# Attention scores of seven pairs of query tiles by seven half-size products, on one Trainium2 core

## The chip, the core and the metric

The kernel runs on one NeuronCore of a Trainium2 chip. The core has five engines with instruction queues of their own: TensorE (PE, matrix products; its weight loads are listed apart as PEld), VectorE (DVE), ScalarE (ACT), GpSimd (POOL) and SyncE (SP, which here only issues DMAs). They work out of an on-chip memory (SBUF); products of TensorE land in an accumulator memory (PSUM), of which the attention uses eight banks, each a tile of 128x512 FP32 values. DMA engines move data between SBUF and the large memory (HBM). The metric is the device time of one execution in microseconds (us). Before the change it is 1065.05 us, the median of three runs (1064.25 to 1067.31).

## What is computed

The input x has 2 batches of 2048 rows of 512 values, all FP32. Cut to what matters:

```python
xn = layernorm(x)
z  = layernorm(xn)                               # once more, with gamma and beta
q, k, v = z @ qkv[:, :512], z @ qkv[:, 512:1024], z @ qkv[:, 1024:]
scores  = q @ k.T / sqrt(512)                    # per batch, causal
s = softmax(where(causal, scores, -inf)) @ v @ o_proj + xn
g = silu(moe(xn))                                # 8 experts, the best 2 per row
out = x + s * g
```

The kernel folds the projections, so that "q" below is already multiplied with the key weights and "v" with the output projection: scores are products of q with the normalised rows ("k"), and the attention's output is the product of the exponentials with "v", divided by their sum.

## The kernel before

The work is in stages, one after the other. First the rows are normalised and q and v made (some of it by a seven-product scheme in `seven_products`, L383), and stored in HBM with k. Then the mixture of experts runs over 68 tiles of gathered rows (`experts_step`, L934; its rows y go to HBM). Then comes the attention, which this change is about.

Attention runs over 32 query tiles of 128 rows, in the order `seq` (L810): tiles 15 down to 0 of the first batch, then the second batch's in the order 8, 9, 0, 1, 6, 7, 2, 3, 4, 5, 10 to 15. A position in that order is called s, and positions 2n and 2n+1 are a pair, two neighbouring tiles. Keys come in blocks of 512; a tile needs all whole blocks before its own and a part of its own block. With the keys of four blocks (NBB = 4) a tile needs 1 to 16 groups of 128 keys (`place_keys`, L1079).

The order of all instructions is written out by hand: the schedule is manual, so each engine takes its instructions in the order in which the code issues them. The loop at L1314 goes over the steps s. In step s it issues, in this order: the ends of older tiles (`attended`, L1252, on ACT and DVE; `emit`, L1263, on POOL, with the store on SP), loads of their inputs, the scores of tile s (`chunk_scores`, L961, one per block of keys: four matmuls that accumulate over the four groups of 128 features into a PSUM tile of the pool `ps_a`, five of the banks; then on DVE the causal mask on the last 128 columns and the maximum along the row) mixed with the joins of tile s-1, then the negated maximum (`end_scores`), `combine_p`, `divisor`, `exponentials(s)`, and the product with the values for an older tile.

`exponentials` (L1031) makes the exponentials of a tile on ACT, out of the PSUM tiles into a buffer `pr`, with the row sums. They have to be transposed for the product with v: POOL splits each FP32 block into 16-bit halves (`pu`, L1045), a DMA on SP transposes them (`puT`, L1050), and DVE joins the halves again (`join_p`, L1065) in the tile's buffer `turned[s]`. Tiles with up to three groups of keys are transposed on TensorE instead (`turn_p`).

For the pairs in FAST = (0, 1, 2, 3, 13, 14, 15) the product with the values already goes by seven half-size products in place of eight (Strassen's scheme in Winograd's form): over two rows of tiles, two halves of each pair of key groups, and two halves of the 512 output columns. `combine_v` (L1100) makes the sums of v, `combine_p` (L1114) those of the exponentials, both on DVE; `values_first`, `values_next` and `values_end` (L1161, L1174, L1181) make the products in the three banks of the pool `ps_b` and add them up on DVE. Key groups beyond the 2m that both tiles have in pairs are done in the plain way (`product`, L1083). m is at most 7 before the change. The first half of a pair's values runs two steps after its scores, the second three.

The first steps take over from the experts: the scores of tile 0 are issued before the last five expert steps, `exponentials(0)` in step 0, and the loads of v on SP in steps 0 and 1, into memory that the experts' weights held. `gather_y` (L1230) fetches the experts' rows by index on POOL, `gate` (L1240) weighs them on DVE and puts them through Silu on ACT.

## Time and profile before

| | |
|---|---|
| median of three runs | 1065.05 us |
| profiled execution | 1064.85 us |
| its span, first to last instruction | 1063.1 us |
| TensorE busy | 1047.8 us, 99% of the span |
| VectorE busy | 592.9 us, 56% |
| ScalarE busy | 312.1 us, 29% |
| GpSimd busy | 419.2 us, 39% |
| granted TensorE clock | 0.999 |
| first and last score product | 591.4 and 1019.6 us |

The page has one line per group of instructions: source line, engine, operation, the output and input by the program's names, their shape, the count, then busy time and mean duration, and the idle time before them with what ended it. A product of FP32 operands is issued once in the code and shows as two records on PE: four matmuls of a block are eight records. The records of PE overlap (their ends are modelled), so their mean is longer than the time from one to the next; that time is read from their starts. Timelines give the start and the duration of each instruction or of a run of like ones.

### The profile page before, as it was taken

What the parts mean: (1) busy time and instruction counts of PE and PEld (TensorE: products, weight loads), DVE (VectorE), ACT (ScalarE), POOL (GpSimd) and SP (SyncE); (2) the same over time, 40 slices, a digit from 0 to 9 for tenths busy, and PEclk for the clock granted to TensorE, in tenths of its full rate; (3) what the DMA queues carried; (4) which work ended last, traced back from release to release, by engine and by line L of the source; (5) the groups of instructions that cost most, each with busy time, mean ns of one, the idle gap of its engine ahead of it and who ended that gap; (6) DMA issues with size and microseconds to landing.
All of it is one profiled execution on the core that took longest, in us unless ns stands there. A gap on an engine that the chain in (4) does not pass through costs nothing.

```text
span 1063.1 us, 12108 instructions
## 1 busy us (share of the span) xinstructions
PE 1047.8 (99%) x3578; PEld 619.9 (58%) x3578; DVE 592.9 (56%) x1175; ACT 312.1 (29%) x665; POOL 419.2 (39%) x457
## 2 busy tenths in 40 slices
PE   8999999999999999999999999999999999999998
PEld 3688885444555555555545446676764544547677
DVE  5798885775433333333345338545556568565756
ACT  3222321212332222322355131222333443332330
POOL 2364250003433333333331024244447676773452
PEclk9999999999999999999999999999999999999999
DMA  8699999936999999999885186346568768752451
GB/s 292 187 286 290 284 263 356 338 112 174 221 236 224 228 231 222 234 229 221 216 190 133 35 227 151 92 104 176 125 170 251 251 189 228 196 152 72 113 138 39
DMA packets 300511, 209.32 MB, mean 197 GB/s; under 512 B 234520, under 2 KB 247576, under 8 KB 299424
## 3 DMA queue, kind: packets, MB, share of 16 engines
q1 hardware_dynamic: 281248, 146.12, 55.2%
q0 software_dynamic: 10560, 35.17, 12.7%
q10 hardware_dynamic: 8640, 27.27, 7.1%
q8 instruction: 30, 0.49, 0.2%
q14 instruction: 33, 0.27, 0.1%
HBM read 92.89 MB, written 60.03 MB: 144 GB/s over the span
## 4 chain that ended last, share of the span: by engine, by line
PE 82%; DMA 4%; issue 4%; POOL 4%; DVE 3%; ACT 2%; SPq 1%; ACTq 0%; POOLq 0%; DVEq 0%
PE ps L966 18%; PE ph L882 15%; PE py L921 15%; PE p L1140 10%; PE p L400 7%; PE po L1087 5%; PE pj L341 3%; PE pj L346 3%; PE pw L207 2%; PE p L1087 2%; DMA puT<-pu 1%; DMA zuT<-zu 1%; POOL yg L1234 1%; POOL pu L1045 1%; DMA v<-v_d 1%
## 5 line engine op out<-in xcount | busy, mean ns | idle before, releaser
L966 PE MATMUL ps<-k,q 128*128 128x512 f32 (+3 forms) x640 | 239.1, 529 | 0.0
L966 PEld LDWEIGHTS ps<-k,q 128*128 128x128 f32 x640 | 117.2, 190 | 119.7 <-issue 109.8
L921 PE MATMUL py<-w,ht 128*128 (+3 forms) x408 | 187.0, 593 | 0.0
L882 PE MATMUL ph<-w,xT 128*128 (+1 forms) x544 | 173.1, 460 | 0.7 <-POOL keep L1004 0.7
L1045 POOL COPY pu<-pr 128x1024 uint16<-128x1024 uint16 (+2 forms) x74 | 80.0, 1111 | 171.9 <-ACT pr L1038 149.4
L929 DVE COPY y<-py 128x512 f32<-128x512 f32 x68 | 46.9, 689 | 177.7 <-PE py L921 177.7
L907 ACT ACTIVATE ht<-ht,b1sel 128x128 f32<-128x128 f32 (+3 forms) x237 | 73.1, 375 | 231.2 <-DVE ht L901 231.2
L882 PEld LDWEIGHTS ph<-w,xT 128*128 128x128 f32 (+1 forms) x544 | 97.4, 181 | 74.1 <-issue 35.2
L892 POOL COPY hu<-h 128x704 uint16<-128x704 uint16 x68 | 52.2, 768 | 206.9 <-ACT h L890 151.9
L921 PEld LDWEIGHTS py<-w,ht 128*128 128x128 f32 (+3 forms) x408 | 73.5, 182 | 75.3 <-issue 37.6
L768 POOL DMA_INDIRECT xs<-zu_d,toki x68 | 69.0, 1014 | 69.3 <-DVE toki L642 57.9
L1038 ACT ACTIVATE pr<-ps,nm 128x512 f32<-128x512 f32 (+3 forms) x80 | 49.0, 620 | 148.3 <-DVE ri L1218 126.2
L972 DVE TENSOR_REDUCE mx<-ps 128x1 f32<-128x512 f32 (+3 forms) x80 | 48.6, 608 | 69.9 <-PE ps L966 68.7
L1234 POOL DMA_INDIRECT yg<-y_d,posi x64 | 67.9, 1062 | 40.4 <-DVE g L1245 23.4
L1087 PE MATMUL po<-v,pT 128*128 128x512 f32 x182 | 81.2, 593 | 1.1 <-ACT pT L1063 1.1
L264 POOL COPY zu<-z 128x1024 uint16<-128x1024 uint16 x32 | 35.2, 1099 | 77.1 <-DVE z L249 77.1
L1069 DVE COPY pT<-puT 128x1024 uint16<-128x1024 uint16 (+2 forms) x74 | 54.2, 740 | 20.0 <-DMA puT<-pu 20.0
L1087 PEld LDWEIGHTS po<-v,pT 128*128 128x128 f32 x182 | 34.2, 190 | 39.5 <-issue 36.1
L1258 DVE SCALAR_TENSOR_TENSOR o<-xo,xscale,o 128x512 f32<-128x512 f32 x30 | 26.9, 906 | 50.0 <-ACT o L1255 43.0
L842 DVE COPY xT<-xhT 128x1024 uint16<-128x1024 uint16 x68 | 46.5, 684 | 13.4 <-DMA xhT<-xs 8.4
L413 DVE TENSOR_TENSOR so<-p,so 128x512 f32<-128x512 f32 x70 | 45.7, 685 | 14.1 <-DMA v_d<-so 8.0
L1266 POOL TENSOR_TENSOR o<-o,g 128x512 f32<-128x512 f32 x30 | 41.3, 1377 | 14.8 <-DVE o L1258 14.6
(219 smaller groups left out, 1447.8 us busy)
## 6 DMA issues: line engine op xcount, KB each, us to landing
y_d<-y SPq DMA_DIRECT2D x68, 256.0 KB, 3.7
zu_d<-zu SPq DMA_DIRECT2D x32, 264.0 KB, 6.4
x<-in_x_dram SPq DMA_DIRECT2D x32, 256.0 KB, 5.4
kt_d<-kT ACTq DMA_DIRECT2D x8, 1024.0 KB, 5.1
k<-kt_d SPq DMA_DIRECT2D x32, 256.0 KB, 4.2
q<-qt_d SPq DMA_DIRECT2D x32, 256.0 KB, 3.8
v<-v_d SPq DMA_DIRECT2D x32, 256.0 KB, 5.2
xo<-in_x_dram SPq DMA_DIRECT2D x32, 256.0 KB, 3.3
```

What stands on the lines that cost most here:

```text
L400: nc.tensor.matmul(ps[:, r, :], lhsT=lhs[:, c, ts(r, P)], rhs=rhs[:, c, :], start=(c == 0), stop=(c == 1),)
L768: nc.gpsimd.indirect_dma_start(out=xs, out_offset=None, in_=zu_d, in_offset=bass.IndirectOffsetOnAxis(ap=toki[:, i : i + 1], axis=0),)
L882: nc.tensor.matmul(ph[at, :], lhsT=xT[:, c, at], rhs=rhs[k], start=(c == 0), stop=(c == ND - 1),)
L892: nc.gpsimd.tensor_copy(hu[:, :, :H], h.bitcast(U16).rearrange("p (d h) -> p h d", h=2))
L907: nc.scalar.activation(ht[:hn, c, at], ht[:hn, c, at], AF.Silu, bias=b1sel[:hn, c, j : j + 1])
L921: nc.tensor.matmul(py[at, :], lhsT=ht[:k, c, at], rhs=rhs[n], start=(c == 0), stop=(c == NH - 1),)
L966: nc.tensor.matmul(ps[:, :w], lhsT=aqs[seq[s] // 2][:, c, ts(t % 2, P)], rhs=aks[first + j][:, c, :w], start=(c == 0), stop=(c == ND - 1),)
L1045: nc.gpsimd.tensor_copy(pu[:, : 2 * w].rearrange("p (h d) -> p h d", h=2), pr[:, :w].bitcast(U16).rearrange("p (d h) -> p h d", h=2),)
L1069: nc.vector.tensor_copy(turned[s][:, j * TB : j * TB + w].bitcast(U16).rearrange("p (i t h) -> p i t h", t=P, h=2), halves[s][j][:, : 2 * ...
L1087: nc.tensor.matmul(dst, lhsT=turned[s][:, ts(k, P)], rhs=avs[first + k // BT][:, k % BT, cols], start=(start and k == k0), stop=(k == k1 - 1),
L1140: nc.tensor.matmul(dst, lhsT=a[:, k], rhs=v(k), start=(k == 0), stop=(stop and k == n - 1))
L1234: nc.gpsimd.indirect_dma_start(out=y, out_offset=None, in_=y_d, in_offset=bass.IndirectOffsetOnAxis(ap=posi[k][:, n : n + 1], axis=0),)
```

## The change

For the pairs in FAST, the scores of both tiles with the first two blocks of keys are made together in the new `fast_scores`. Seen as matrices they are a product of 2x2 parts: two query tiles by two halves of the 512 features, times two halves of the features by two blocks of 512 keys. Seven products of 256 features each replace eight; each is two matmuls of 512 columns, so that the pair's sixteen matmuls for these blocks become fourteen. The products leave PSUM by one copy and seven additions into `turned[s]` and `turned[s+1]`, where the sums stand as plain scores; the exponentials later overwrite them in place. `query_sums` (four sums of the pair's q) and `block_sums` (four sums of the two blocks, once per batch) make the operands. Blocks after the first two, and all tiles outside FAST, go through `chunk_scores` as before.

With it go:

- `pr` and its pool are gone: exponentials go straight to `turned[s]`, which is now one of four buffers (s modulo 4), taken at the start of the step (`room`).
- The maximum of the two first blocks is one reduction over 1024 columns, and their exponential one activation.
- First steps: only blocks 2 and 3 of tile 0 are scored before the last expert steps; then blocks 2 and 3 of tile 1, the fast scores of pair 0, the exponentials of both tiles. Step 1 issues no product. Step 2 holds the fast scores of pair 1. The values of pair 0 run in step 3 as a whole.
- All four blocks of v are loaded in step 0 (before: two in step 0, two in step 1). q is fetched one pair ahead, at the start of each even step, into two buffers (before: three).
- m is at most 6 (`MOST`), so the last block of v needs no sums; pairs 0 and 15 (keys 16 and 15) do one more pair of key groups in the plain way.
- `gather_y` fetches a pair at once into a buffer that `gate` then works in; for the last pair it is issued in step 31, after that step's `emit`s (before: in step 30).
- Four small tiles of the first stage move to another pool, `xo` has four buffers in place of five, and a scratch tile of the end shares the gather's.

```diff
+    def query_sums(s, engine):
+        q = qsums[s] = sq.tile([P, 4, ND // 2, P], F32, name=f"sq_{s}", tag="sq")
...
+        engine.tensor_tensor(q[:, 0], a21, a22, ALU.add)
+        engine.tensor_tensor(q[:, 1], q[:, 0], a11, ALU.subtract)
+        engine.tensor_tensor(q[:, 2], a11, a21, ALU.subtract)
+        engine.tensor_tensor(q[:, 3], a12, q[:, 1], ALU.subtract)
+
+    def block_sums(first):
+        k = bsums[first] = kt.tile([P, 4, ND // 2, TB], F32, name=f"tk_{first}", tag="tk")
...
+        nc.vector.tensor_tensor(k[:, 0], b12, b11, ALU.subtract)
+        nc.vector.tensor_tensor(k[:, 1], b22, k[:, 0], ALU.subtract)
+        nc.gpsimd.tensor_tensor(k[:, 2], b22, b12, ALU.subtract)
+        nc.vector.tensor_tensor(k[:, 3], b21, k[:, 1], ALU.subtract)
+
+    def fast_scores(s, pools, meanwhile=()):
...
+        p1 = made(a11, b11)
+        if s == 2:
+            nc.vector.tensor_copy(c11, p1)
+        else:
+            nc.scalar.copy(c11, p1)
+        p2 = made(a12, b21)
+        add(c12, made(q[:, 1], k[:, 1]), c11)
+        add(c11, p2, c11)
+        add(c21, made(q[:, 2], k[:, 2]), c12)
+        p5 = made(q[:, 0], k[:, 0])
+        add(c22, p5, c21)
+        add(c12, p5, c12)
+        others(1)
+        add(c12, made(q[:, 3], b22), c12)
+        others(1)
+        add(c21, made(a22, k[:, 3]), c21)
+        maximum(s, turned[s][:, : 2 * TB], 0)
+        others(len(meanwhile))
...
-    begin_scores(0)
-    for j in range(len(widths[0])):
+    for s in range(2):
+        begin_scores(s)
+    for j in direct(0):
         chunk_scores(0, j)
...
-            pr = pp.tile([P, TB], F32, name=f"pr_{s}_{j}", tag="pr")
             nc.scalar.activation(
-                pr[:, :w], chunks[j][:, :w], AF.Exp, bias=nm, accum_out=rs[:, j : j + 1]
+                turned[s][:, at:end], src, AF.Exp, bias=nm, accum_out=rs[:, j : j + 1]
             )
...
-        m = min(place_keys(s), place_keys(s + 1)) // 2
+        m = min(min(place_keys(s), place_keys(s + 1)) // 2, MOST)
...
-        xt = op.tile([P, D], F32, name=f"xo_{s}", tag="xo", bufs=5)
+        xt = op.tile([P, D], F32, name=f"xo_{s}", tag="xo", bufs=4)
...
+        n = s // 2 + 1
+        if s % 2 == 0 and NQ <= n < NT // 2:
+            for c in range(2):
+                fetch_q(n, c)
+        if s == 0:
+            fetch_parts(s, NBB * ND)
+            block_sums(0)
...
+        if s == NT - 1:
+            gather_y(NT - 2)
...
+        if s < NT and s % 2 == 0 and len(pair) == 2:
+            pools = [(ps_b, "b")] * (NBB - 1) + [(ps_a, "a")] if s < 3 else [(ps_a, "a")]
+            fast_scores(s, pools, [joins.pop(0) for _ in joins[:2]])
+            if s == 0:
+                query_sums(2, nc.gpsimd)
+        for k, j in chunks:
+            chunk_scores(k, j)
...
+            if s % 2 == 0 and len(pair) == 2:
+                maximum(s + 1, turned[s + 1][:, : 2 * TB], 0)
+            if s == 0:
+                end_scores(1)
+                exponentials(1)
...
+            if s == 23:
+                block_sums(K)
+            if s % 2 and s > 3 and s // 2 + 1 in FAST:
+                query_sums(s + 1, nc.vector)
...
+        elif s == 3:
+            values_first(0)
+            values_next(0)
+            for f, *args in joins:
+                f(*args)
+            values_end(0, [lambda: query_sums(s + 1, nc.vector)])
```

## The prediction

> **What bounds the kernel now.** I read the page's engine shares first, then what TensorE waited for, then the groups by shape.

> ```profile
> PE 1047.8 (99%) x3578; PEld 619.9 (58%) x3578; DVE 592.9 (56%) x1175; ACT 312.1 (29%) x665; POOL 419.2 (39%) x457
> PE p L1140 <- DVE s L1131: 2.1, 1, 2.1
> PE p L1140 <- DVE vT L1112: 0.3, 1, 0.3
> PE py L921 <- DVE w2c L869: 0.9, 1, 0.9
> L966 PE MATMUL ps<-k,q 128*128 128x512 f32 x448 | 196.7, 593 | 0.0
> ```

> PE is busy 1047.8 of 1063.1 us, and after the kernel's start its list of waits has some 6 us in all, the longest of them 2.1 where the attention's first values begin (L1140, on the sums of exponentials). Everything else is hidden behind PE, so a product removed is time removed, if none of the new work makes PE wait. The price of a product is not the mean of 593 ns, as records overlap. It is read from the weight loads of the scores, one per record:

> ```profile
> 700.72 0.19 PEld L966 LDWEIGHTS ps<-k,q 128*128 128x128 f32 x1 [0.24 <-issue]
> 701.15 0.19 PEld L966 LDWEIGHTS ps<-k,q 128*128 128x128 f32 x1 [0.24 <-issue]
> 701.58 0.19 PEld L966 LDWEIGHTS ps<-k,q 128*128 128x128 f32 x1 [0.24 <-issue]
> 691.07 0.95 DVE L1131 TENSOR_TENSOR s<-pT 128x768 f32<-128x768 f32 x1
> 695.11 2.75 PE L1140 MATMUL p<-vT,s 128*128 128x256 f32 x12
> 719.40:753.40 34.00, 34.00 (x131) 24.02 (x131) 18.45 (x38) 9.11 (x18) 14.82 (x14) 1.00 0.56 146
> ```

> They start 0.43 us apart: 0.86 us for a matmul of 512 columns (two records). Twelve records of 256 columns take 2.75 us with the overlap of the last, 0.215 each, 0.43 per matmul. The next two lines show a narrow place of a fast pair: DVE had the first sum of exponentials ready at 692.0, PE began to use it at 695.1, 3.1 us later. The last line, from the table of stretches, gives a pair's 34 us of step time: PE full, DVE busy 18.45, ACT 9.11, POOL 14.82.

> [...] the same 768-column sum takes 0.95 us, and 1.67 while POOL copies. [...]

> **Removed.** Per pair sixteen matmuls of 512 columns become fourteen: 2 x 0.86 = 1.72 us, times seven pairs **-12.04 us**, all on PE, which sets the end. **Added on PE:** m falls from 7 to 6 for pairs 0 and 15. Seven half products (256 columns) of one m become eight: one more, 0.43 each, **+0.86**.

> **Added on DVE.** Seven additions out of PSUM per pair; the same form in the projections (so<-p,so, 128x512) takes 0.685: 4.8 us. Four sums of q of 256 columns at 0.42: 1.7. Four maxima at 0.687 go and two over 1024 come (1.2 by the slope of the rows for 128, 256 and 512, 292, 424 and 687 ns): -0.3. In sum +6.2 per pair: 18.45 becomes 24.7 of 32.3 us, still not the bound. The block sums cost DVE 3 x 1.22 and POOL one of twice 1.30 us, twice in the kernel, once beside the last experts' products and once in step 23. There PE works on values whose inputs were joined a step earlier; without that cover DVE's part would cost 3.7. ACT gets one copy (0.58) per pair. In its place the pair's two first exponentials become one instruction per tile, which saves two accumulator reads of 0.2. The first two query sums are on POOL: 4 x 0.65 (half of 1.30 for 512). The first lies among the experts, where POOL works 1.8 of some 5 us; the second begins when pair 0's sixth product is read and ends at most 1 us after its seventh, while pair 1 needs it 3.4 us after.

> **An even step of a fast pair, from the end T of the products before it.** ACT stands behind the older pair: last addition 0.4, DVE's `gate` 2.5 (719.77 to 722.2), Silu 1.06, two `attended` 1.5, then the copy of the first product 0.6: T+6.0. PE makes a product each 1.72, has five banks, and needs the copied bank for the sixth at T+8.6: 2.6 us to spare. DVE's two final sums of the older pair end at T+6.7, and its additions begin 1.5 us behind PE. They catch up at the fifth and sixth product (0.69 and one join of 0.68 per 1.72). The last ends at T+13, the maximum at T+14.2. In step 4 the block left comes off PE at T+15.5, its mask and maximum take 1.0, two joins 1.1, the negation 0.15, the first sum of exponentials 0.95: T+18.8. PE is at T+12.04 with the products, T+15.5 with the block left, T+21.5 with `values_first` (14 x 0.43): 2.7 us to spare; 2.5 in step 6, more in 28 and 30. So no stall, in the forecast.

> **The first steps.** PE's end with the last expert moves from 615.5 to 608.5, as only eight matmuls of tile 0 stand before it (the w2c wait of 0.9 stays: the same reduction is in front of it). Two blocks of tile 1 take 6.0, pair 0's products 12.0: T1 = 626.5. Then PE has 12.0 for pair 1, 5.2 and 4.3 for the rest of tiles 2 and 3 (512 and 256, 512 and 128 columns by four): it reaches pair 0's values at T1+21.5. Until then run: last addition, maximum, negation (T1+2.4), exponentials of both tiles (to 8.5), eight splits on POOL at 1.2 (to 12.6), transposes (3.2 from the end of a split to its join, as for the first tile before, 617.2 to 620.5), joins. puT has five buffers, so the last three transposes wait for joins, which stand in DVE's queue between pair 1's additions and its maxima: the eighth lands at some T1+20.2 and is joined at 21.2. Tile 0's four are joined at 18.6, so `values_first` (6.9) isn't held. Step 3's v sums and the first sum of exponentials come at T1+27, and PE asks at 28.4. From there DVE has thirteen sums in one row (sums of exponentials 1.0, of v 0.55 to 1.1) up to T1+37.3, then the addition that frees the bank of `values_first`: 38.1; PE wants the bank at 36.4. Stall 1.8. Before, this place lost 2.1 + 0.3, and another 0.8 in pieces (`values_next` took 656.8 - 649.7 = 7.1 for 14 x 0.43): 3.2. **-1.4.** What DVE waited for longest in the attention, and SP's queue there, before:

> ```profile
> DVE pT L1069 <- DMA puT<-pu: 20.0, 11, 7.6
> 623.48 10.36 SPq L794 DMA_DIRECT2D v<-v_d  x16
> ```

> The 7.6 us is at 632.8 to 640.4: transposes stood behind the v loads in SP's queue. The loads now start by 609 and are over by 620; the first transpose is asked for at 630.

> **The end.** The last gathers now stand behind four emits on POOL (5.6 us) and before the last four splits, which end 44 us after step 30 begins; the joins and four sums behind them free a PSUM bank at about 53, where PE asks at 52.2: **+0.9.**

> Query loads one pair ahead land (3.8 us) a step and a half before use: nothing; uncovered 3.8 per pair. Four xo buffers: the load waits for an emit that SP's store ahead of it waits for too. Nothing.

> **Sum:** -12.04 + 0.86 - 1.4 + 0.9 = -11.7. The profiled execution, 1064.85 with 1.75 around its span, becomes 1053.2; the median shown is 0.2 higher: **1053.4 us**. Bounds of what the trace doesn't show: additions at 0.60 (back-to-back pitch) leave the sum as it is[...]; the first steps lie between no stall (-1.8) and 6 us more, if the eighth transpose and the sums behind it come one POOL backlog late.

> **Rivals.**
> A, back into new waits: DVE and ACT are 2 to 4 us later per pair than I walked, or the first steps lose 5 to 8. For it: margins of only 2.5 us, DVE busy at 76%. Against: DVE catches up inside each pair. Gives back 3 to 8: 1056.5 to 1061.9.
> B, slower: the chain copy - additions - maximum - sums becomes the bound of each fast pair. Place: DVE between T and `values_next`. Its stall must be (11.7 + 3.2)/7 = 2.1 us per pair; with 2.5 to spare, it decides from 4.6 us of delay per pair on, 23.4 instead of 18.8. Speaks for it: the copy stands behind Silu, which stands behind a gather on POOL. Against: in the trace the gather lands before `gate`, and DVE never waited for it. At 6 us of delay: 3.5 x 7 = 24 lost, 1078.
> C, the products save nothing, since halves of 256 features cost more than half (a start and end per bank). The projections' seven products stream 56 records of 256 columns in 12.28 us, 0.219, no gap. Time 1065; hardly.

> **How the numbers follow.** Forecast 66% (1051 to 1056.5), A 20%, B 9%, C and other ways to no change 5%. A measurement tells 0.3%, 3.2 us: faster 0.66 + 0.20 = 0.86, same 0.05, slower 0.09. Leaving out B, C and thin edges (above 1060.5 and under 1050.5, 3% each) the range is 1050.5 to 1060.5.

> **What would show it.** PE's busy time down by 11.2. Under the seven pairs' products 98 matmuls in runs of 28 records of about 12.0 us, with no wait; a wait for DVE or ACT inside them is A or B. The copy of the first product at T+6. The first sum of exponentials ahead of `values_next` by over 2 us; if not, A. One wait of some 2 us before `values_end`'s second bank near 663. If v loads or transposes end waits on DVE in step 2, the first steps are wrong.

## The result, and the profile after

The changed kernel takes **1072.94 us** (median, 1072.02 to 1076.03), the kernel before 1065.05; the ratio is 1.0077, with a 95% interval of 1.0055 to 1.0099. It is slower, where 1053.4 was forecast with a chance of 0.86 for faster. Its profiled execution took 1073.81 us, with a span of 1072.1, 9.0 more than the span before.

The engine shares of the page of the changed kernel, and below them the longest rows of its list of what TensorE waited for (total us, times, longest us; the row of L307 belongs to the first stage, the others to the attention):

```profile
PE 1044.4 (97%) x3554; PEld 619.0 (58%) x3554; DVE 647.9 (60%) x1229; ACT 311.9 (29%) x643; POOL 431.1 (40%) x467
```

```profile
PE p L1232 <- DVE s L1223: 4.7, 2, 4.5
...
PE po L1183 <- DVE pT L1165: 3.3, 1, 3.3
PE po L1183 <- ACT pT L1161: 3.1, 1, 3.1
...
PE pg L307 <- DVE zT L290: 2.3, 1, 2.3
```

PE's busy time fell by 3.4 us and not by 11.2, and in the attention waits of 3 to 4.5 us stand where before none was over 2.1. The products themselves came out as priced. Groups by shape, weight loads and a table row of the changed kernel (columns as in the prediction):

```profile
L994 PE MATMUL ps<-k,q 128*128 128x512 f32 x224 | 99.9, 593 | 0.0
```

```profile
723.08 0.19 PEld L1044 LDWEIGHTS p<-k,q 128*128 128x128 f32 x1 [0.24 <-issue]
723.51 0.19 PEld L1044 LDWEIGHTS p<-k,q 128*128 128x128 f32 x1 [0.24 <-issue]
...
719.00:753.00 34.00, 34.00 (x135) 24.80 (x134) 24.61 (x45) 7.87 (x14) 15.94 (x16) 1.00 0.58 149
```

The whole products went from 448 records to 224. In steps 6 and 7 a record of the half-size ones starts every 0.43 us, PE is full, and DVE's 24.6 us of 34 is the forecast 24.7. The loss is elsewhere. This is PE's timeline of the changed kernel at the places where it waited (start, length, records; in brackets the idle time before them and what ended it):

```profile
662.42 5.49 PE L1232 MATMUL p<-vT,s 128*128 128x256 f32 x12 [4.53 <-DVE s L1223]
667.71 2.83 PE L1232 MATMUL p<-vT,pT 128*128 128x256 f32 x12
...
830.01 2.84 PE L1183 MATMUL po<-v,pT 128*128 128x512 f32 x6 [3.06 <-ACT pT L1161]
...
921.53 6.53 PE L1183 MATMUL po<-v,pT 128*128 128x512 f32 x8 [3.30 <-DVE pT L1165]
...
938.50 1.98 PE L1044 MATMUL p<-k,sq 128*128 128x512 f32 x4 [1.85 <-ACT pT L1063]
...
967.35 1.98 PE L1044 MATMUL p<-k,sq 128*128 128x512 f32 x4 [1.11 <-ACT pT L1063]
```

Two rows carry more than their wait: twelve records of 256 columns took 5.49 us at 662, where the next twelve took 2.83, and eight of 512 took 6.53 at 921, where eight take 3.60. The table of stretches shows why (its columns from the left: stretch, length, busy time of PE, weight loads, DVE, ACT, POOL; then the granted clock of TensorE, third from the right):

```profile
664.00:666.00 2.00, 2.00 (x7) 1.55 (x5) 2.00 (x2) 1.34 (x2) 2.00 (x3) 0.50 0.26 53
923.00:925.00 2.00, 2.00 (x3) 0.67 (x2) 0.94 (x2) 1.02 (x4) 1.93 (x3) 0.50 0.75 231
```

After the rests of 4.53 and 3.30 us the clock (1.00 is the full one) was 0.50, half clock from here on, for the first 5.4 and 5.7 us of work. PE counts as busy there, which hides 2.7 and 2.9 us of loss in its busy time.

Cut at points that PE reaches in the same order, the spans compare as follows (us; the three columns on the right are after minus before). "Expert wait" is PE's wait of 0.9 for w2c, in front of which the kernel before has 6.88 us more of tile 0's scores; "transposed tile" is the first tile with transposes on PE, "its values" the row at 830.01.

| stretch | forecast | measured | with the three edits below |
|---|---|---|---|
| start to expert wait, without the 6.88 | 0 | +2.6 | +0.7 |
| expert wait (and 6.88) to transposed tile | -7.9 | -0.8 | -5.9 |
| transposed tile to its values | 0 | +1.9 | -0.8 |
| its values to pair 26's products | 0 | +6.5 | 0.0 |
| pair 26's products to pair 30's | -3.4 | +0.1 | -0.3 |
| pair 30's products to the end | -0.4 | -1.3 | -1.3 |
| sum | -11.7 | +9.0 | -7.5 |

### The profile page after: what moved, and what is told of

The parts are those of the page before. It is cut to its first block, busy times and chain, and to the rows that moved or that the text cites. A ratio compares the mean times of both kernels' runs of the same rounds, so it can differ in the third digit from the quotient of the medians.

```text
span 1072.1 us, 12190 instructions
## 1 busy us (share of the span) xinstructions
PE 1044.4 (97%) x3554; PEld 619.0 (58%) x3554; DVE 647.9 (60%) x1229; ACT 311.9 (29%) x643; POOL 431.1 (40%) x467
## 4 chain that ended last, share of the span: by engine, by line
PE 77%; DVE 7%; issue 6%; POOL 5%; ACT 3%; DMA 2%; SPq 0%; ACTq 0%; POOLq 0%; DVEq 0%
PE py L921 15%; PE ph L882 15%; PE p L1232 10%; PE ps L994 8%; PE p L400 7%; PE p L1044 6%; PE pj L341 3%; PE pw L207 3%; PE po L1183 3%; PE pj L346 3%; PE p L1183 2%; DVE vT L1205 2%; DMA zuT<-zu 1%; DVE pT L1165 1%; POOL yg L1329 1%
## 5 line engine op out<-in xcount | busy, mean ns | idle before, releaser
L921 PE MATMUL py<-w,ht 128*128 (+3 forms) x408 | 187.1, 594 | 0.0
L994 PE MATMUL ps<-k,q 128*128 128x512 f32 (+3 forms) x416 | 143.0, 495 | 0.0
L1144 POOL COPY pu<-pT 128x1024 uint16<-128x1024 uint16 (+2 forms) x74 | 83.2, 1153 | 133.3 <-ACT pT L1136 70.5
L921 PEld LDWEIGHTS py<-w,ht 128*128 128x128 f32 (+3 forms) x408 | 73.4, 182 | 75.4 <-issue 37.4
L994 PEld LDWEIGHTS ps<-k,q 128*128 128x128 f32 x416 | 74.7, 190 | 67.6 <-issue 58.4
L1183 PE MATMUL po<-v,pT 128*128 128x512 f32 x182 | 84.2, 611 | 6.4 <-DVE pT L1165 3.3
L1329 POOL DMA_INDIRECT yg<-y_d,posi x64 | 64.8, 1012 | 47.0 <-DVE yg L1340 32.7
L1136 ACT ACTIVATE pT<-ps,nm 128x512 f32<-128x512 f32 (+3 forms) x52 | 30.0, 580 | 65.5 <-DVE nm L1080 40.0
L1358 POOL TENSOR_TENSOR o<-o,yg 128x512 f32<-128x512 f32 x30 | 42.1, 1405 | 12.7 <-DVE o L1350 12.6
L1136 ACT ACTIVATE pT<-pT,nm 128x1024 f32<-128x1024 f32 x14 | 16.1, 1149 | 104.3 <-DVE nm L1080 75.0
```

Source lines behind the costliest of these rows:

```text
L921: nc.tensor.matmul(py[at, :], lhsT=ht[:k, c, at], rhs=rhs[n], start=(c == 0), stop=(c == NH - 1),)
L994: nc.tensor.matmul(ps[:, :w], lhsT=aqs[seq[s] // 2][:, c, ts(t % 2, P)], rhs=aks[first + j][:, c, :w], start=(c == 0), stop=(c == ND - 1),)
L1144: nc.gpsimd.tensor_copy(pu[:, : 2 * w].rearrange("p (h d) -> p h d", h=2), turned[s][:, k : k + w].bitcast(U16).rearrange("p (d h) -> p h ...
L1183: nc.tensor.matmul(dst, lhsT=turned[s][:, ts(k, P)], rhs=avs[first + k // BT][:, k % BT, cols], start=(start and k == k0), stop=(k == k1 - 1),
L1329: nc.gpsimd.indirect_dma_start(out=y, out_offset=None, in_=y_d, in_offset=bass.IndirectOffsetOnAxis(ap=posi[k][:, n : n + 1], axis=0),)
```

## Experiments

The theory after the result: three hand-overs, of which the prediction walked only the first, come late, each through a queue of its own (DVE in step 3, the Silu's table load on ACT, the block sums on DVE in step 23), and a long rest of PE (4.53 and 3.30 us here) is followed by half clock. Rival one: DVE has too much work in all, so that what one edit gives back is lost a step later. Rival two: the half-size products save less than 1.72 us per pair.

**v sums ahead of the last join.** DVE's timeline of the changed kernel at the wait of 4.53:

```profile
654.16 0.69 DVE L1165 COPY pT<-puT 128x1024 uint16<-128x1024 uint16 x1 [4.22 <-DMA puT<-pu]
...
656.82 3.97 DVE L1205 TENSOR_TENSOR vT<-v 128x512 f32<-128x512 f32 x3
...
661.42 0.95 DVE L1223 TENSOR_TENSOR s<-pT 128x768 f32<-128x768 f32 x1
```

DVE idled 4.22 us for the eighth transpose, and then made PE wait for three sums that need no transpose. SP's queue of the changed kernel shows the rest of it:

```profile
633.48 14.10 SPq L1149 DMA_TRANSPOSE puT<-pu  x8
```

The v loads no longer stand in front of the transposes, as the prediction had it, and the longest wait fell from 7.6 to 4.2; but eight transposes stand in one row. The eighth was issued at 646.34, and its last part landed 7.7 us later. The three sums were moved in front of the last join:

```
-            if s == 3:
-                if j == 2:
-                    for b in range(NBB - 1):
-                        combine_v(b, (1,))
-            elif joins:
+            if s != 3 and joins:
...
-            for f, *args in joins:
+            while joins:
+                if s == 2 and len(joins) == 1:
+                    for b in range(NBB - 1):
+                        combine_v(b, (1,))
+                f, *args = joins.pop(0)
```

> Only the order on DVE changes: step 3's first three sums of v stand before the last join of step 2, where DVE waited 4.22 us for a transpose, not behind that join. Theory 'three late hand-overs, and a half clock after a long rest of PE': the first sum of exponentials comes 4.0 us earlier (658.4 for 662.4), PE's wait of 4.5 us at pair 0's values falls to 0.5, and the 12 records behind it take 2.75 and not 5.49: 6.5 us faster than the changed kernel, 1066.4. Rival 'DVE has too much work in all, so what is saved here is lost a step later': 1071 to 1073.

Measured: ratio to before 1.0054 (1.0041 to 1.0067), median 1072.19. PE's timeline of this kernel:

```profile
664.24 2.86 PE L1232 MATMUL p<-vT,s 128*128 128x256 f32 x12 [1.55 <-DVE vT L1205]
668.90 1.56 PE L1183 MATMUL p<-v,pT 128*128 128x256 f32 x6 [1.80 <-DVE o L1249]
...
916.54 6.77 PE L1183 MATMUL po<-v,pT 128*128 128x512 f32 x8 [3.30 <-DVE pT L1165]
```

The wait of 4.5 and its half clock are gone. Two waits of 1.55 and 1.80 came up behind it in the same row of DVE's sums, so the stretch from pair 0's values to step 4 is 28.06 for 32.64 us, 4.6 shorter and not 6.5. The ratio is 0.23%, 2.4 us, below that of the changed kernel, and the intervals overlap; the trace places the effect, the timing doesn't size it.

**Block sums behind gate.** In step 23 of the changed kernel DVE had:

```profile
906.77 1.21 DVE L1022 TENSOR_TENSOR tk<-k,k 128x1024 f32<-128x1024 f32 x1
908.01 1.94 DVE L1023 TENSOR_TENSOR tk<-k,tk 128x1024 f32<-128x1024 f32 x1
909.99 3.25 DVE L1025 TENSOR_TENSOR tk<-k,tk 128x1024 f32<-128x1024 f32 x1
```

6.4 us for three sums, and behind them gate, its Silu, `attended` and the join that PE's values wait for.

```
-            if s == 23:
-                block_sums(K)
...
+        if s in (21, 23):
+            block_sums(K, (0, 1) if s == 21 else (2, 3))
```

The new place is behind gate; all four sums are on DVE.

> The second batch's four block sums go from step 23's middle (before gate, one of them on POOL) to behind gate in steps 21 and 23, two each, all on DVE. Theory of the hand-overs: DVE was 6.4 us with them in front of gate, so the wait of 3.3 us at 918 to 921.5 goes (0 to 1 left), and with it the slow records (6.53 becomes 3.60): 5.5 to 6.3 us faster than the changed kernel, 1066.6 to 1067.4. Rival 'DVE's load as a whole': the wait turns up at the next values or inside pair 26, 1071 to 1073.

Measured: 1.0019 (1.0003 to 1.0035), median 1068.59; by the ratios 6.2 us faster than the changed kernel, as the theory had it. PE's timeline of this kernel:

```profile
916.30 3.60 PE L1188 MATMUL po<-v,pT 128*128 128x512 f32 x8
```

The values start without a wait and take 3.60 us. The stretch from the transposed tile's values to pair 26 is 93.06 for 97.89, and 1.7 of those 93.06 are a new half clock behind the unchanged rest of 3.06 at 826.67. Pair 26's wait grew from 1.85 to 2.38, half a microsecond of the rival's kind.

**The block sums in place, none on POOL**, to tell contention from place:

```
-        nc.gpsimd.tensor_tensor(k[:, 2], b22, b12, ALU.subtract)
+        (nc.vector if first else nc.gpsimd).tensor_tensor(k[:, 2], b22, b12, ALU.subtract)
```

> Only the engine of one of the second batch's four block sums changes, POOL to DVE; they stay in step 23 in front of gate. Theory 'place and contention both': alone on its operands DVE needs 4 x 1.22 = 4.9 us where it took 6.4 beside POOL, gate comes 1.5 us earlier, the wait of 3.3 falls to 1.8 and with it the half clock goes: 4.4 faster than the changed kernel, 1068.5. Rival 'contention isn't it, the four sums are late by place alone': no gain, 1072 to 1074.

Measured: 1.0079 (1.0053 to 1.0105), median 1075.23, no gain. DVE's timeline of this kernel:

```profile
912.67 1.21 DVE L1024 TENSOR_TENSOR tk<-k 128x1024 f32<-128x1024 f32 x1
913.81 1.21 DVE L1025 TENSOR_TENSOR tk<-k,tk 128x1024 f32<-128x1024 f32 x1
```

Four sums now take 5.4 us where three took 6.4, so the contention is real, and PE's rest went from 3.30 to 2.28. But the eight records behind it still took 5.40 for 3.60, at half clock, and the transposed tile's values had half clock too (4.29 for 2.84). So contention cost about 1 us of the rest and the place the other 2.28; the half clock was expected to end with a rest below 3 us, and it did not.

**The Silu's table load.** ACT's timeline of the kernel before, and under it that of the changed kernel, at the same gate:

```profile
818.67 1.28 ACT L1250 ACT_TABLE_LOAD   x1
820.56 1.06 ACT L1250 ACTIVATE g<-g 128x1024 f32<-128x1024 f32 x1 [0.60 <-DVE g L1246]
```

```profile
822.51 1.28 ACT L1342 ACT_TABLE_LOAD   x1 [1.95 <-DVE yg L1340]
823.80 1.06 ACT L1342 ACTIVATE yg<-yg 128x1024 f32<-128x1024 f32 x1
```

Before, the table was loaded while ACT waited for gate's sums; now the load itself waits for them, in each of the fourteen gates from the third on, where before it did so in one of sixteen. Why isn't shown: the Silu overwrote its input before as well, and what differs is that gate's sums now stand in the gathered tile (`yg`) and not in a tile of their own (`g`). A Silu of one column, with nothing to wait for, was put in front of gate's sums, so that the load could run before them:

```
         g, *ys = rows.pop(s)
+        early_silu = sm.tile([P, 1], F32, name=f"es_{s}", tag="es", bufs=1)
+        nc.scalar.activation(early_silu, ident[:, :1], AF.Silu)
```

> A Silu of one column of a constant stands in front of each gate on ACT, so that the table load (1.28 us) runs before gate's sums and not behind them, where the change had put it ([...]the load itself waits for DVE). Theory 'table loads in the hand-overs': the wait of 3.06 at 830 falls to 1.8, that of 3.30 at 921.5 to 2.0 and its slow records go (-2.9), those of 1.85 and 1.11 in pairs 26 and 28 fall to 0.6 and 0: 7.9 us faster than the changed kernel, 1065. Rival 'the load is hidden, the waits come from DVE alone': 1072 to 1073.

Measured: 1.0010 (0.9997 to 1.0022), median 1067.68; by the ratios 7.1 us faster than the changed kernel, for 7.9 expected. It is the lowest ratio of the single edits, though its interval overlaps that of the block sums. PE's timeline of this kernel:

```profile
827.44 2.84 PE L1183 MATMUL po<-v,pT 128*128 128x512 f32 x6 [0.31 <-ACT pT L1161]
...
916.42 3.70 PE L1183 MATMUL po<-v,pT 128*128 128x512 f32 x8 [0.88 <-DVE pT L1165]
...
926.94 6.80 PE L1044 MATMUL p<-tk,sq 128*128 128x512 f32 x12 [3.39 <-DVE sq L1014]
```

The load at the gate shown above ran at 819.29, behind no wait, and gate's Silu at 821.27, where only 0.49 us of ACT's wait for the sums was left. PE's 3.06 fell to 0.31 and 3.30 to 0.88, more than the load's 1.28 each. At the first place Exp's load behind it on ACT, which had waited to 827.73, ran at 823.01; at the second the join took 0.68 us, where it had taken 1.47. But DVE then stood 3.73 us for a transpose in step 25 and made pair 26's query sums late: 3.39 of rest and half clock inside the products. Here the rival is half right: what one hand-over gave back, the next one partly took.

**Work added in PE's rests.**

```
+        if s == 0:
+            for _ in range(8):
+                nc.tensor.matmul(p57[:, LO], lhsT=ident, rhs=avs[0][:, 0, LO], start=True, stop=True)
...
+        if s == 23:
+            for _ in range(2):
+                nc.tensor.matmul(po, lhsT=ident, rhs=avs[place(s)[2]][:, 0, :], start=True, stop=True)
```

The first stands before the products of `values_next`, the second before those of `values(23)`; both results are overwritten.

> Work added, none removed: eight matmuls of 256 columns (3.4 us) whose result is overwritten, before pair 0's values_next, and two of 512 (1.7 us) before the values of step 25, both inside PE's two longest waits (4.5 and 3.3 us). Theory 'half clock after a rest of more than some 3.2 us': both runs of slow records go, 5.6 us faster than the changed kernel, 1067.3, with the same sums on DVE late. Rival 'records were slow for another reason': 1072 to 1073, or up to 5 us more if PE wasn't free there.

Measured: 1.0074 (1.0053 to 1.0095), median 1074.38, no gain in all, where 5.6 us had been expected. At the two places it did what the theory says: the stretch with pair 0's values is 31.0 for 32.6 us with 3.4 us of products added, and the values at 925 run at full clock (3.70) behind a rest of 1.58. In the profiled execution the half clock came elsewhere instead, behind a rest of 2.38 in pair 26 and behind the transposed tile's rest, as long as before:

```profile
831.03 5.49 PE L1186 MATMUL po<-v,pT 128*128 128x512 f32 x6 [3.06 <-ACT pT L1161]
```

The theory's 3.2 us was an estimate from the changed kernel's rests, 3.06 without half clock and 3.30 with it; here 2.38 and 3.06 were enough.

Why the median of eleven runs shows no gain is not settled by this one execution.

**The three edits together**, v sums, block sums and Silu:

> The three single edits together: v sums before the last join of step 2, the second block sums behind gate in steps 21 and 23, the early Silu. If the losses are separate hand-overs they add: step 3 loses 3.4 instead of 8.0 (waits of 1.6 and 1.8, no slow records), the transposed tile 0.3 for 3.1, step 25 none of its 6.2, pairs 26 and 28 some 0.6 for 3.0; together 15.9 off the changed kernel: 1057. Rival 'DVE's load in all': as after the Silu alone, new waits of 3 us turn up, 1062 to 1066.

Measured: **1058.76 us, 0.9936 (0.9920 to 0.9951) of before**: faster than both kernels, and by the ratios 15.0 us faster than the changed one, for 15.9 expected. So the losses add, and rival one falls for most of them; but pair 26's products took 14.8 us, for 14.1 in the changed kernel, and there some was lost again. The three longest of what this kernel's PE still waits for in the attention:

```profile
PE p L1188 <- DVE o L1254: 1.8, 1, 1.8
PE p L1237 <- DVE vT L1210: 1.5, 1, 1.5
PE p L1049 <- ACT pT L1068: 1.1, 1, 1.1
```

No rest is over 1.81, and the clock is 1.00 all through the attention.

**Step 3 ordered further**, on top: six v sums early, and pair 0's sums of exponentials in front of tile 3's maxima.

```
+                        combine_v(b, (1, 3))
...
+            if s == 2:
+                combine_p(0, range(NBB - 1))
             if s % 2 == 0 and len(pair) == 2:
                 maximum(s + 1, turned[s + 1][:, : 2 * TB], 0)
```

> The same, and step 3 ordered further: six of the twelve v sums (the first and the third of each block) before the last join, and pair 0's sums of exponentials in front of tile 3's maxima. Theory: the first sum is ready at PE's time, no wait left at pair 0's values but one under 1 us: 2.5 below the kernel with three edits, 1054.5, so 0.9 to 1.0% faster than before. Rival: tile 3's maxima, now 10 us later, make PE wait in step 4 or 6; then no gain on the kernel with three edits.

Measured: 0.9962 (0.9950 to 0.9974), median 1061.11, slower than with three edits. The first sum came in time, but PE waited 4.50 us for the addition that frees the bank of `values_first`, with half clock behind: 30.6 us for the stretch from pair 0's values to step 4, where three edits took 28.1. ACT's timeline of this kernel:

```profile
666.03 1.15 ACT L1141 ACTIVATE pT<-pT,nm 128x1024 f32<-128x1024 f32 x1 [10.48 <-DVE nm L1085]
...
668.18 0.37 ACT L1265 COPY p<-p 128x256 f32<-128x256 f32 x1
```

The copy that this addition needs stands behind tile 3's exponentials on ACT, and these waited 10.48 us for the maxima that had been put off. With three edits the same copy ran at 656.07. Neither theory nor rival had named this.

**Only the six v sums early**, the rest of step 3 as it was:

> The kernel with three edits, with six v sums in place of three (the first and the third of each block) before the last join of step 2, and the sums of exponentials left behind tile 3's maxima, as they were. With three edits PE waited 1.53 for a v sum and 1.81 for the addition that frees the bank of values_first, all 2 to 4 us behind in one row on DVE. Theory: the row gets three sums shorter, the first wait goes, the second falls to 0 to 1: 1.5 to 3 us faster than with three edits, 1056.5. Rival (the last join is late by as much as is saved, as with step 3 ordered further): 1058 to 1060.

Measured: 0.9961 (0.9947 to 0.9975), median 1063.1. The wait of 1.53 went, one of 0.61 for the first sum came, and that for the addition grew from 1.81 to 2.74, with half clock: 29.7 us for this stretch, for 28.1, which is 1.6 of the 2.7 us that this kernel loses by the ratios. As the rival said, the last join was late by about as much as was saved.

**Whole products in pairs 13 to 15** (the kernel with step 3 ordered further otherwise), to price the half-size products:

```
+    SCORE = FAST[:4]
...
-        return range(2 if s // 2 in FAST else 0, len(widths[s]))
+        return range(2 if s // 2 in SCORE else 0, len(widths[s]))
```

> The kernel with step 3 ordered further, but pairs 13 to 15 get their scores by whole products as before (no block sums of the second batch, no query sums there). This prices the half-size products where nothing waits. Theory 'each pair saves PE 1.72 us': three pairs give 5.2 us back, less some 0.6 of waits in their products: 4.6 slower than the same kernel with all seven pairs, 1059. Rival 'the half products save little, the additions make up for it': 0 to 2 slower.

Measured: 0.9989 (0.9976 to 1.0001) for 0.9962, 2.9 us slower by the ratios (4.0 by the medians), between the 4.6 of the theory and the 0 to 2 of the rival. The traces give 1.6, within the width of the intervals: from pair 26 to the end the kernel with half-size products took 144.3 us, the one with whole products 145.9, so three pairs saved 1.6 where 5.2 had been forecast. Their products tell why: pair 30's took 12.0 us, as priced; pair 28's 12.4; pair 26's 14.7. So rival two falls where nothing waits, and pair 26 loses 2.7 us of what the second batch saves.

**Gate and `attended` behind the additions** in steps 26 and 28, on the kernel with six v sums early:

```
+            if s in (26, 28):
+                gate(s - 4)
+                finish(s)
```

This stands behind the fast pair's products, and `gate` leaves steps 25 and 27 for it; `finish` holds the loop with `attended` and `emit`, which stays at the head of the other steps.

> The same, and in steps 26 and 28 gate, attended and emit of the older pair stand behind the fast pair's additions and first maximum on DVE and ACT, not in front of the copy of the first product. Theory 'what stands ahead of that copy is what pairs 26 and 28 lose' (2.7 and 0.4 us left with three edits): both pairs' products take 12.0 us, 2.5 to 3 us faster than the kernel without this, 1053.8. Rival: the older pair's outputs come 12 us later, a PSUM bank of values or a split on POOL waits for them and PE with it: no gain.

Measured: 1.0000 (0.9988 to 1.0012), median 1065.32, slower than the kernel that it changes (1.0000 for 0.9961). Pair 26's products took 12.8 us for 15.2, so what stood ahead of the copy was the cause of most of its loss. But the work put off made pair 28's query sums late: a rest of 2.39, then twelve records in 7.11 us for 5.31, and a rest of 2.72 before pair 26's values.

**Query sums at the head of the step** (on the kernel with three edits):

```
+        if s in (25, 27, 29):
+            query_sums(s + 1, nc.vector)
```

They stand in front of the step's maxima.

> The kernel with three edits, with the query sums of pairs 26, 28 and 30 on DVE at the head of the step before (25, 27, 29), where DVE then waits 2 us for a transpose, not at its end in front of gate. Left in pair 26 are waits of 0.23, 1.10 and 0.71 and 0.7 in pieces, 2.7 us. Theory 'what stands ahead of the copy of the first product': gate, Silu and the copy come 2 to 2.7 us earlier, pair 26's products take 12.0 to 12.7 us in place of 14.8, pair 28's 12.0: 2 to 2.5 faster, 1056.5. Rival: the mask and maxima now 1.7 us later hold up the exponentials or the gathers, no gain.

Measured: 0.9942 (0.9928 to 0.9957), median 1059.59, no difference from the three edits that the intervals could tell. In the trace pair 26's products take 13.5 us for 14.8, but the copy is still late by 1.20, and a rest of 2.02 before pair 0's values had half clock in this execution.

**The four small tiles alone**, moved in the kernel before:

```
-    gw = const.tile([P, ND, GW], F32, name="gw")
+    gw = mp.tile([P, ND, GW], F32, name="gw")
...
-    sc = const.tile([P, E, NT], F32, name="sc")
+    sc = mp.tile([P, E, NT], F32, name="sc")
```

> The kernel before with nothing but the four small tiles moved to the other pool, as the change has them. It tells whether the 2.6 us that the changed kernel's profile was behind before anything else of the change is reached belong to the change. Theory 'the start varies from execution to execution, whatever the kernel': 1065 to 1066, no difference that can be measured. Rival 'the new places of these tiles cost it': 1067.5 to 1068.5.

Measured: 1.0011 (0.9998 to 1.0023), no difference. Between the profiled executions of the changed kernel and those made from it, which share all code up to there, PE reaches the expert wait anywhere from 600.7 to 609.7 us. The +2.6 of the table's first row is within this, so no cause in the change is needed for it. Much of it is one wait of the first stage (L307): 0.7 us in the kernel before, 2.3 in the changed one, and 0.2 to 5.5 in the kernels made from it.

## Why the prediction was wrong

**Held.** The price of a product, 0.43 us a record and 12.0 us a pair: shown in pairs 0 to 6 and 30. DVE's load per pair (its 49 additions out of PSUM took 0.677 to 0.693 us each, for 0.685). The even steps 4 and 6, where the copy of the first product ended at T+6.0, as forecast, and nothing waited. m going from 7 to 6. The start of pair 0's values, at T1+21.5 as walked.

**"The end", +0.9**: it was 0. No wait for a PSUM bank turned up; the stretch gained 1.3, which is 1.72 less 0.43.

**"The first steps", -1.4: the step that failed first.** Two of its terms were too small. The eighth transpose was put at T1+20.2 and its join at 21.2. It was issued at T1+17.0, which fits the walk, but landed after 7.7 us and not 3.2 (5.2 to 7.7 over the profiled executions of this kernel and those made from it), and its join ended at T1+25.5. The row behind it was given 5.8 us up to the first sum of exponentials and took 7.5, because the three v sums took 1.3 us each, twice their 0.67, while POOL split tile 2. So the sum was ready at T1+33 and not at 27. The prediction had the mechanism and a bound for it, 6 us more, but not the order: it left three sums standing behind a join that they don't need. With them moved this place lost 3.4 us, for 8.0 in the changed kernel and 1.8 in the forecast (whose own figures, 38.1 less 36.4, give 1.7).

**"In step 23 PE works on values whose inputs were joined a step earlier; without that cover 3.7."** The cover was looked for at the wrong work. What stood behind the block sums was gate, then on ACT the Silu and `attended`, then on DVE again the addition of xo and the join of tile 23, with the values of that tile two steps on. And 3.7 was 6.4, beside POOL's sum of 3.31 us. The prediction had a sum slowed beside POOL in its own trace (768 columns, 0.95 us and 1.67), but priced these without it, at 1.22, which is what the slope of that trace's sums gives for 1024 columns (L1131: 0.95 us at 768, 1.08 to 1.09 at 896). Cost: 3.3 of rest and 2.9 of half clock. The sums were one link of this chain and the table load another: with the early Silu alone, and the sums where they were, the rest was 0.88.

**Not in the prediction: the wait on the table load.** That gate works in the gathered tile was left without a price. With the change a wait of ACT moved from the Silu to the table load in front of it, 1.28 us in each gate from the third pair on. The copy of a transposed tile, the copy of the first product in pairs 26 and 28, and the join in step 25 all stand behind such a Silu. For pairs 26 and 28 the "T+6.0" was T+10.5 and T+9.8.

**Not in the prediction: the clock.** Each rest was priced at its length. Two of them cost 1.6 and 1.9 times that.

**The rivals.** B was the side that came true, but not its mechanism: no fast pair's own chain of additions was the bound, and the delay of 4.6 us per pair from which it should decide was nearly reached in pair 26 alone, whose copy was 4.5 us late. A's shape (margins lost in hand-overs) fits, but it allowed 3 to 8 us given back, and 18 were, without the start's 2.6. C is refuted by pair 30.

Open: why the eighth transpose took 7.7 us to land (SP issued the loads of q and xo right behind it; that they slowed it isn't shown); how much the v sums alone gain, which the timing can't tell from nothing, as it can for the block sums behind gate and for the early Silu; why the table load took over the Silu's wait; and what else keeps pair 26's copy late. A kernel that orders step 3 further without holding back that copy on ACT was not tried.

## What to carry to other kernels

When an engine that is busy for 99% of the span gets shorter work, walk not only the steps that are edited but every queue in which new work now stands: ask for each added instruction what is behind it two steps on, and put it where its engine already waits. Here a change of buffers came with a wait on the table load in front of the Silu (1.28 us each, in fourteen gates of sixteen), so look at what each table load or copy waits for. And price a rest of TensorE of 2 us or more with half clock behind it: 18 of the 24 such rests in these traces had it.

## What the runs showed of the hardware

Half clock after a rest, over the 14 profiled executions, rests of PE in the attention from 1.5 us on:

| rest | rests | followed by clock 0.50 |
|---|---|---|
| 1.53 to 1.85 us | 10 | 0 |
| 2.02 to 3.10 us | 16 | 10 |
| 3.30 to 4.53 us | 8 | 8 |

```profile
824.87:828.28 3.41, 2.08 (x14) 1.36 (x12) 2.25 (x6) 1.20 (x2) 3.31 (x4) 1.00 1.04 383
828.28:831.69 3.41, 1.68 (x4) 0.87 (x5) 0.98 (x3) 2.35 (x5) 3.10 (x3) 1.00 0.94 251
```

```profile
826.60:830.00 3.40, 1.37 (x12) 1.18 (x10) 2.23 (x6) 1.25 (x1) 3.32 (x3) 1.00 0.94 346
830.01:833.42 3.41, 2.38 (x3) 1.17 (x4) 1.62 (x7) 1.86 (x6) 2.39 (x3) 0.50 0.95 216
```

DVE's block sums beside POOL in the changed kernel: the three of the first batch, 1024 columns each, took 1.21 to 1.23 us (from 611.91 on), where POOL had nothing to do; in step 23 the first took 1.21, and the two behind it 1.94 and 3.25 beside POOL's copy and its own sum. POOL's sum, estimated at 2.6 from the 1.30 us that it took for 512 columns before the change (L376), took 3.31 us there and 2.35 in the first batch, where DVE made none beside it.
